# Several parts of the last image under way at once in the normalisation, the inverse DFT and the token layers

## The chip, the cores and the metric

The kernel runs as one program on one core of a Trainium2 chip. A core has a matrix engine (PE, with its weight loads shown as PEld), a vector engine (DVE), an activation engine (ACT), a general engine (POOL) and a queue engine (SP), which here issues all transfers between the memory of the chip (DRAM) and the on-chip buffer (SBUF). PE writes its results into PSUM, eight banks of 512 float32 per partition; DVE and ACT read them from there. The metric is the time of one execution on the device in microseconds.

## What is computed

The input is 4 images of 64 x 64 points with 96 channels. Four layers follow one another: two with a scan along the image in four directions, two with attention and a feed-forward part on the 4096 points as tokens.

```python
x = x + L0(group_norm(x))      # 192 inner channels
x = x + irfft2(L1(rfft2(x)))   # 64 x 33 frequencies, 384 inner channels
t = x.reshape(4, 4096, 96)
for layer in (2, 3):
    t = t + attn(norm(t)); t = t + ffn(norm(t))
# L0, L1: xz = x @ W; conv 3x3; silu; four scans with 16 states;
#         y = norm(sum of the four + skip) * silu(z); y @ out_w
# attn: q, k, v of 6 heads; ((q k^T) * 16**-0.5) v, no softmax; @ Wff + bff
# ffn: float8 (5 exponent bits, 2 of mantissa) factors, float16 sums,
#      relu between the two products
```

As attention has no softmax, the products can be taken in another order: the kernel forms one 97 x 97 matrix G = Xn^T Xn over all tokens of the image (96 channels and a column of ones), and from it and the weights one 97 x 96 matrix `wo`. Each token then needs only `xn @ wo`. G needs every normalised token before the first token can go on.

## The kernel before

`build` (line 1203) first prepares the first pair of images, then runs `scans` (line 480), which walks through all the scan steps of both scan layers: two phases for layer 0 (image pairs) and four for layer 1 (one image each). In `scans` the instructions of PE, DVE, ACT and POOL stand in an order written out by hand. The other work, for instance the normalisation after a scan, the inverse DFT and the token layers of an earlier image, runs as side tasks: generators that `Env.step` (line 83) moves on by one step where `slot` finds room. `E.defer` puts an eviction at the head of the next step.

When the scans of image 3 are through, nothing is left to run beside what still has to be done for that image: `alone(tail, end1, 3).finish()` (line 1288). This environment has `wide=4` and a PSUM pool of eight banks under one tag; the side tasks in the scans have `wide=1` and one bank. Outside the scans the order of the instructions in each engine's queue is set by a planner, which takes the code's order as priority. `end1` (line 1260) does three things one after another:

- `Block.gated` (line 350). The 33 rows of frequencies come in blocks of 8, 8, 6, 6 and 5 (`cfg.rows`), and a block in tiles of two rows. `load` (line 364) brings a tile: the scan results of the two row-wise directions `yt[:, 0]`, of the two column-wise ones `yt[:, 1]` by one transfer per row, and the scan's input `ut`; two tiles are buffered. Per tile PE multiplies `ut` with the skip weights (line 394) and adds the transposed four directions in the same bank (line 400), and ACT copies the bank into the block's `y` (line 410). Per block follow the mean by a product on PE (414), the subtraction on DVE (417), the square on ACT (420), the variance on PE (424), logarithm and exponential on ACT (427, 428), two multiplications on DVE (431, 436), and `out1` (line 899): for each row three products with `wo` (912), a copy for two rows (919), one store for the block into `att` (921). The buffers `y`, the gate `z` and the square `sq` exist once.
- `inverse` (line 982). Three groups of 32 channels, one after the other: two loads of `att` into `at` (998), 64 products `piv` in four banks (1013) with a copy each (1018), then two banks of `pio` (1029), the addition of the image from before the layer (1032), and the stores to `x1` (1034). The next group's `at` is loaded ahead; `v` exists once.
- `tokens` (line 1041). `x` holds the image as 32 tiles of 128 tokens. For each of the two layers: eight weight loads (1107 to 1118) with casts to float8 (1121, 1123); `layer_norm` (1058) over all tokens in four parts of eight tiles, the parts overlapping one another; G (`pg`, 1128) and the small products to `wo` (`small`, 1098); attention in eight groups of four tiles (transposition `pt` 1149, copy `xt` 1151, product `pao` 1155, addition 1157); the second `layer_norm`; the feed-forward part in eight groups (transposition `ptf` 1164, cast `x8` 1166, three products `ph` 1172 with copies 1173, bias and relu 1176, cast `h8` 1179, product `pfo` 1184, copy `y16` 1192, two additions 1194 and 1198). At the end one store of the whole image (1199).

`together` (line 111) gives several generators one step each in turn. Before, only the preparation of the first pair uses it.

Of the kernel before, what the change touches and what calls it, by code (L numbers as in the profile page):

```python
# [21 lines left out]
C, P = 3, 128  # L22
# [101 lines left out]
class Block:  # L124
# [225 lines left out]
    def gated(self, E, g, io, out_proj):  # L350


        nc, cfg = self.nc, self.cfg
        yn, yo = io["y"][cfg.nat], io["y"][1 - cfg.nat].rearrange("k (w r) c -> r w k c", r=cfg.NR)
        u, gz = io["u"][cfg.nat], io["gz"]
        with E.pool(f"{cfg.pre}nm{g}") as sp:
# [3 lines left out]
            tiles = [  # L360
                (b, i, r + i, min(2, n - i)) for b, (r, n) in enumerate(cfg.rows) for i in range(0, n, 2)
            ]

            def load(b, i, r, n):
                nm = f"{cfg.pre}_{g}_{r}"
                yt = sp.tile([P, 2, 2, C * P], F32, name=f"yt_{nm}", tag="yt", bufs=2)
# [5 lines left out]
                ut = sp.tile([P, C, P], F32, name=f"ut_{nm}", tag="ut", bufs=2)  # L372
                nc.sync.dma_start(out=ut[:, :, : n * 64], in_=u[:, :, r * 64 : (r + n) * 64])
                return yt, ut

            todo = iter(tiles)
            nxt = load(*next(todo))
            yield
            yield
            yield  # L380
            for b, (r, nr) in enumerate(cfg.rows):
                n = nr * 64
                nm = f"{cfg.pre}_{g}_{r}"
                z = sp.tile([P, C, 512], F32, name=f"zb_{nm}", tag="zb")
                nc.sync.dma_start(out=z[:, :, :n], in_=gz[:, :, r * 64 : r * 64 + n])
                y = sp.tile([P, C, 512], F32, name=f"yb_{nm}", tag="yb")
                for i in range(0, nr, 2):
                    m = min(2, nr - i) * 64
                    yt, ut = nxt
                    more = next(todo, None)  # L390
                    nxt = load(*more) if more else None
                    ps = E.psum(f"py_{nm}_{i}")[:, : C * P].rearrange("p (c t) -> p c t", c=C)
                    for c in range(C):
                        nc.tensor.matmul(
                            ps[:, c, :m], self.skip[:, c, :], ut[:, c, :m], start=(c == 0), stop=False
                        )
                    yield
                    for c in range(C):
                        for k in range(4):
                            nc.tensor.matmul(  # L400
                                ps[:, c, :m],
                                yt[:m, k // 2, k % 2, c * P : (c + 1) * P],
                                self.ident[:m, :m],
                                start=False,
                                stop=(c == C - 1 and k == 3),
                                is_transpose=True,
                            )
                        if c < C - 1:
                            yield
                    E.defer(lambda i=i, m=m, ps=ps, y=y: nc.scalar.copy(y[:, :, i * 64 : i * 64 + m], ps[:, :, :m]))  # L410
                    yield
                pm = E.psum(f"pm_{nm}")
                for c in range(C):
                    nc.tensor.matmul(pm[:, :n], self.mean_w, y[:, c, :n], start=(c == 0), stop=(c == C - 1))
                    yield
                for c in range(C):
                    nc.vector.tensor_tensor(y[:, c, :n], y[:, c, :n], pm[:, :n], ALU.subtract)
                yield
                sq = sp.tile([P, C, 512], F32, name=f"sq_{nm}", tag="sq")
                nc.scalar.activation(sq[:, :, :n], y[:, :, :n], AF.Square)  # L420
                yield
                pv = E.psum(f"pv_{nm}")
                for c in range(C):
                    nc.tensor.matmul(pv[:, :n], self.mean_w, sq[:, c, :n], start=(c == 0), stop=(c == C - 1))
                    yield
                ln = sp.tile([P, 512], F32, name=f"ln_{nm}", tag="ln")
                nc.scalar.activation(ln[:, :n], pv[:, :n], AF.Ln, bias=self.eps)
                nc.scalar.activation(pv[:, :n], ln[:, :n], AF.Exp, scale=-0.5)
                yield
                for c in range(C):  # L430
                    nc.vector.scalar_tensor_tensor(
                        y[:, c, :n], y[:, c, :n], self.lnw[:, c : c + 1], pv[:, :n], ALU.mult, ALU.mult
                    )
                yield LATE
                for c in range(C):
                    nc.vector.scalar_tensor_tensor(
                        y[:, c, :n], y[:, c, :n], self.lnb[:, c : c + 1], z[:, c, :n], ALU.add, ALU.mult
                    )
                yield
                yield from out_proj(E, sp, wo, y, r, nr)  # L440
# [429 lines left out]
def out0(images, ins, x0):  # L870


    def task(E, blk, sp, wo, y, r, nr):
        nc = E.nc
        PI = blk.cfg.PI
        tok = slice(r * 64, (r + nr) * 64)
# [105 lines left out]
def inverse(E, cst, att, x, b, x1):  # L982
# [5 lines left out]
    with E.pool(f"fi{b}") as sp:  # L988
# [5 lines left out]
        def load(c0):  # L994
            a = sp.tile([2 * HH, WP, G], F32, name=f"at_{b}_{c0}", tag="at", bufs=2)
            nc.gpsimd.memset(a[:, WF:, :], 0.0)
            for r in range(2):
                nc.sync.dma_start(
                    out=a[r * HH : (r + 1) * HH, :WF, :], in_=att[:, :, r * CH + c0 : r * CH + c0 + G]
                )  # L1000
            return a

        nxt = load(0)
        yield
        yield
        for c0 in range(0, CH, G):
# [395 lines left out]
```

## Time and profile before

| what | value |
|---|---|
| runs | 12100.39, 12104.8, 12110.57 us; median 12104.8 |
| profiled execution | 12108.82 us, of which its span is 12106.9 |
| mean granted PE clock | 0.87 of full |
| PE busy | 9441.0 us (78% of the span) |
| DVE busy | 10572.7 us (87%) |
| ACT busy | 9071.5 us (75%) |
| POOL busy | 8900.0 us (74%) |
| DRAM traffic | 1221.74 MB read, 236.50 MB written |

The page of the profile gives the busy time of each engine, also as digits in 40 equal slices of 302.7 us (a 9 is 90% busy or more; PEclk is the clock granted to PE in tenths). A window cuts out a stretch of microseconds from the span's start. A row of the timeline has the start, the length, the engine, the line of the code, the operation, output<-input with shapes, the number of merged instructions (x8), and in brackets how long the engine had stood idle before and what ended that. A row of the waits names who waited for whom, with total time, number of times, and the longest. Idle time of an engine that is not on the path to the end costs nothing.

### The profile page before, as it was taken

Reading aid. Unit: us, or ns where it says so; the run is one execution under the profiler, and the core shown is the slowest. Engines: PE = TensorE matmul, PEld = TensorE weight load, DVE = VectorE, ACT = ScalarE, POOL = GpSimd, SP = SyncE. Lnnn points to the kernel's source line nnn. Section 1 sums busy time; section 2 is a strip of 40 time slices with the busy share of each in tenths; the row PEclk is TensorE's granted clock in tenths of the full one; section 3 lists DMA queues with packets and bytes.
Section 4 is the critical chain, followed back from the end, with each engine's and each line's share of the span. In section 5 each row is a group of like instructions: output and inputs, shape, how many; then the busy total and the mean of one; then the engine's idle time right before and its main releaser. Section 6 shows DMA issues by size and latency. Waiting matters only on the chain. (4 is left out here: it accounts for less than half of the span.)

```text
span 12106.9 us, 164888 instructions
## 1 busy us (share of the span) xinstructions
PE 9441.0 (78%) x54800; PEld 6783.4 (56%) x54800; DVE 10572.7 (87%) x10183; ACT 9071.5 (75%) x18534; POOL 8900.0 (74%) x7074
## 2 busy tenths in 40 slices
PE   5677777777788778777888888788778877887765
PEld 2455555555666556556665565565556555565544
DVE  6899999999999999998879888988989899899854
ACT  3778888898778888887667777777777677777733
POOL 2888889888778888987668877877667766676630
PEclk8889999989889989998879889888878877898886
DMA  5554444556555445445543443444224422452231
GB/s 142 123 135 115 119 125 112 134 157 158 146 143 117 129 130 128 129 132 154 144 120 112 130 123 116 152 128 115 85 91 145 118 82 88 135 132 89 82 103 36
DMA packets 1270447, 1469.07 MB, mean 121 GB/s; under 512 B 496023, under 2 KB 1033823, under 8 KB 1260119
## 3 DMA queue, kind: packets, MB, share of 16 engines
q1 hardware_dynamic: 1269591, 1458.53, 44.1%
q8 instruction: 431, 7.06, 0.2%
q14 instruction: 425, 3.48, 0.1%
HBM read 1221.74 MB, written 236.50 MB: 120 GB/s over the span
## 5 line engine op out<-in xcount | busy, mean ns | idle before, releaser
L636 POOL TENSOR_TENSOR hy_l<-du_l,bc_l 128x512 f32<-128x512 f32 (+2 forms) x3456 | 3956.4, 1165 | 2266.6 <-DVE hcy_l L807 1206.7
L789 POOL TENSOR_TENSOR hcx_l<-hx_l,bc_l 128x1024 f32<-128x1024 f32 (+2 forms) x1616 | 3524.5, 2181 | 279.6 <-DVE hx_l L643 244.1
L593 ACT ACTIVATE bx_l<-dut_l,bt_l 128x192 f32<-128x192 f32 (+2 forms) x6272 | 2771.7, 498 | 0.1
L665 PE MATMUL acc_l<-ident,hcx_l 128*128 128x128 f32 (+1 forms) x12000 | 1885.7, 306 | 357.1 <-POOL hcx_l L789 353.3
L665 PE MATMUL acc_l<-ident,hcy_l 128*128 128x128 f32 (+1 forms) x11994 | 1850.5, 302 | 381.9 <-DVE hcy_l L807 378.5
L618 ACT ACTIVATE ax_l<-delta_l,l_alog 128x512 f32<-128x512 f32 (+2 forms) x3456 | 2139.3, 667 | 0.0
L665 PEld LDWEIGHTS acc_l<-ident,hcy_l 128*128 128x128 f32 (+1 forms) x11994 | 1550.1, 156 | 945.6 <-DVE hcy_l L807 571.3
L665 PEld LDWEIGHTS acc_l<-ident,hcx_l 128*128 128x128 f32 (+1 forms) x12000 | 1545.3, 157 | 852.5 <-POOL hcx_l L789 615.0
L807 DVE TENSOR_TENSOR hcy_l<-hy_l,bc_l 128x1024 f32<-128x1024 f32 (+2 forms) x1615 | 1950.7, 1208 | 43.0
L643 DVE TENSOR_TENSOR_SCAN hx_l<-ax_l,state_l,b_l 128x512 f32<-128x512 f32 (+2 forms) x1648 | 1786.8, 1125 | 222.8 <-PE b_l L613 142.1
L643 DVE TENSOR_TENSOR_SCAN hy_l<-b_l,state_l,hy_l 128x512 f32<-128x512 f32 (+2 forms) x1648 | 1789.7, 1121 | 143.8 <-ACT b_l L618 122.4
L618 ACT ACTIVATE b_l<-delta_l,l_alog 128x512 f32<-128x512 f32 (+2 forms) x1912 | 1200.4, 628 | 881.4 <-DVE hx_l L643 839.3
L613 PE MATMUL b_l<-ident,bx_l 128*128 128x128 f32 (+1 forms) x6718 | 1184.5, 303 | 408.3 <-DVE hy_l L643 193.5
L618 ACT ACTIVATE ab_l<-delta_l,l_alog 128x512 f32<-128x512 f32 x1321 | 909.3, 688 | 700.3 <-DVE hx_l L643 668.7
L613 PEld LDWEIGHTS b_l<-ident,bx_l 128*128 128x128 f32 (+1 forms) x6718 | 825.8, 152 | 905.8 <-DVE hy_l L643 296.7
L643 DVE TENSOR_TENSOR_SCAN hy_l<-ab_l,state_l,hy_l 128x512 f32<-128x512 f32 x961 | 1177.1, 1260 | 97.0 <-ACT ab_l L618 62.0
L643 DVE TENSOR_TENSOR_SCAN hx_l<-ax_l,state_l,ab_l 128x512 f32<-128x512 f32 x962 | 1177.5, 1265 | 95.6 <-PE ab_l L613 66.3
L613 PE MATMUL ab_l<-ident,bx_l 128*128 128x128 f32 x5288 | 903.3, 306 | 454.2 <-DVE hy_l L643 218.0
L656 POOL COPY state_l<-hx_l 128x2 f32<-128x2 f32 x1344 | 1114.3, 829 | 0.0
L613 PEld LDWEIGHTS ab_l<-ident,bx_l 128*128 128x128 f32 x5288 | 653.5, 154 | 799.4 <-DVE hy_l L643 298.5
L272 PE MATMUL pc_l<-pad_l,l_dg 128*128 128x512 f32 (+2 forms) x1656 | 796.5, 569 | 77.9 <-ACT uh_l L250 72.2
L176 PE MATMUL pi_l<-xi_l,l_wi 96*128 96x384 f32 (+6 forms) x912 | 469.0, 629 | 248.2 <-DMA xi_l<-xn 94.8
(193 smaller groups left out, 11970.2 us busy)
## 6 DMA issues: line engine op xcount, KB each, us to landing
bc_l<-l_xd_l SPq DMA_DIRECT2D x1536, 256.0 KB
bc_l<-l_xd_l SPq DMA_DIRECT2D x384, 512.0 KB
bc_l<-l_xd_l SPq DMA_DIRECT2D x384, 384.0 KB
us_l<-l_u SPq DMA_DIRECT2D x96, 768.0 KB
l_y<-y_l SPq DMA_DIRECT2D x288, 256.0 KB
bc_l<-l_xd_l SPq DMA_DIRECT2D x192, 320.0 KB
yt_l<-l_y SPq DMA_DIRECT2D x264, 192.0 KB
yt_l<-l_y SPq DMA_DIRECT2D x128, 384.0 KB
```

Of the source, the lines that this page charges most:

```text
L176: self.nc.tensor.matmul(out[i * cfg.PI : (i + 1) * cfg.PI, :n], wi[:, ki, half, :], xin[:, max(i, ki), :n], start=(ki == 0), stop=(ki == c ...
L272: nc.tensor.matmul(pc[:, : n * 64].rearrange("p (r w) -> p r w", w=64), diag[:, t, :], pad[:, r - p0 + dy : r - p0 + dy + n, dx : dx + 64] ...
L593: nc.scalar.activation(t[:n, b, :, ch], z.dut[:n, b, :, ch], AF.Copy, scale=z.bt[:n, b, m : m + 1])
L613: nc.tensor.transpose(pb[:, t : t + n], st.z.bx[st.q, j][:n, b, st.c], ident[:n, :n])
L618: nc.scalar.activation(out, z.delta[:, st.c, : z.S], AF.Exp, scale=z.blk.A[:, st.c, z.k, n : n + 1])
L636: nc.gpsimd.tensor_tensor(st.hy[:, j, :S], st.z.du[:, st.c, :S], st.z.b[st.q][:, j, :S], ALU.mult)
L643: nc.vector.tensor_tensor_scan(h[:, j, : z.S][:, ::step], a[:, : z.S][:, ::step], b[:, : z.S][:, ::step], 0.0 if z.first else z.state[st.c ...
L656: copy(z.state[st.c][:, n0 : n0 + 2].rearrange("p (j o) -> p j o", o=1), h[:, :, e : e + 1])
L665: nc.tensor.matmul(z.acc[st.c][:n, b, :], hc[:, j, t : t + n], ident, start=(n0 + j == 0 and b == 0), stop=(n0 + j == NST - 1 and b == 0), ...
L789: nc.gpsimd.tensor_tensor(hcx[:, :, :S], hx[:, :, :S], z.c[q][0][:, :, :S], ALU.mult)
L807: nc.vector.tensor_tensor(hcy[:, :, :S], st.hy[:, :, :S], z.c[q][1][:, :, :S], ALU.mult)
```

## The change

With `E.wide` over 1, that is for image 3 after the scans alone:

- `gated` is cut into three workers (`W = min(E.wide, 3)`). Worker `w` takes blocks w, w+3; all go in turns through `together`. Each has its own `yt`, `ut`, `zb`, `yb`, `sq`, `ln` and `ab` by a number in the tag, and loads its own next tile ahead.
- `inverse` loads all three channel groups first and runs them in turns, each with its own `v` and `xr`.
- `tokens` is opened before `inverse`, up to its first yield: constants, the ones of `xn` and the weight loads of both layers stand there, in buffers for two layers. The casts of both layers follow after the load of `x`. The tokens go through each layer as four parts of eight tiles (two groups of four): a part does attention for its two groups, its norm, the feed-forward part for its two groups, and, in layer 2, the norm for layer 3; in layer 3 it stores its result. The four parts go in turns. The first norm is done likewise. Between the layers G still needs all parts.

With `wide=1` (images 0 to 2) the steps stay, but for the weights of a token layer, whose eight loads are now issued together ahead of the four casts, and those of layer 2 ahead of the load of `x`; there is one yield more. The PSUM pool, the matrix products and the data moved are as before; the image's store is cut in four.

```diff
     def gated(self, E, g, io, out_proj):
+        W = min(E.wide, 3)
...
-                yt = sp.tile([P, 2, 2, C * P], F32, name=f"yt_{nm}", tag="yt", bufs=2)
+                yt = sp.tile([P, 2, 2, C * P], F32, name=f"yt_{nm}", tag=f"yt{b % W}", bufs=2)
...
+            def worker(w):
+                blocks = list(enumerate(cfg.rows))[w::W]
+                todo = iter([(b, i, r + i, min(2, n - i)) for b, (r, n) in blocks for i in range(0, n, 2)])
+                nxt = load(*next(todo))
+                yield
+                yield
+                yield
+                for b, (r, nr) in blocks:
+                    z = sp.tile([P, C, 512], F32, name=f"zb_{nm}", tag=f"zb{w}")
...
+                    yield from out_proj(E, sp, wo, y, r, nr, w)
+            yield from together([worker(w) for w in range(W)], W)
...
 def inverse(E, cst, att, x, b, x1):
+    W = min(E.wide, CH // G)
...
+        def channels(c0, a, w):
+            v = sp.tile([2 * WP, G, HH], F32, name=f"v_{b}_{c0}", tag=f"v{w}")
...
+        if W > 1:
+            loads = [load(c0) for c0 in range(0, CH, G)]
+            yield from together([channels(w * G, a, w) for w, a in enumerate(loads)], W)
...
 def tokens(E, ins, consts, ident, x1, b, out):
+    A, Q, W = CH + 1, 8, E.wide
...
+        def weights(ly):
+            nm, w, bufs = f"{b}_{ly}", {}, min(W, 2)
...
+                t = w[name] = sp.tile(shape, F32, name=f"{name}_{nm}", tag=name, bufs=bufs)
+                src = ins[f"l{ly}_{name}"]
+                nc.sync.dma_start(out=t, in_=src.to_broadcast([P, CH]) if name == "b2" else src)
+            yield w
+            for name in ("w1", "w2", "b1", "b2"):
+                t = w[name]
+                r = sp.tile(list(t.shape), F8, name=f"q{name}_{nm}", tag=f"q{name}", bufs=bufs)
+                yield LATE
+                nc.vector.tensor_copy(r, t, saturate=False)
...
+        loads = [weights(ly) for ly in (2, 3)]
+        ws = [next(loads[0])] + ([next(loads[1])] if W > 1 else [])
+        yield
         x = sp.tile([P, NT, CH], F32, name=f"tok_{b}", tag="tok")
         nc.sync.dma_start(out=x, in_=x1.rearrange("(p t) c -> p t c", t=NT))
+        yield
+        yield
+        for load in loads[: len(ws)]:
+            yield from load
...
+        def layer_norm(nm, p):
+            t0, w = p * Q, p % W
+            yield LATE
+            s = sp.tile([P, 2, Q], F32, name=f"lns_{nm}_{p}", tag=f"lns{w}")
+            m, v = s[:, 0, :], s[:, 1, :]
+            xs, xq = x[:, t0 : t0 + Q, :], xn[:, t0 : t0 + Q, :CH]
+            nc.vector.tensor_reduce(m, xs, AX.X, ALU.add)
+            nc.vector.tensor_scalar(m, m, 1.0 / CH, None, ALU.mult)
+            nc.vector.tensor_tensor(
+                xq, xs, m.rearrange("p (t o) -> p t o", o=1).to_broadcast([P, Q, CH]), ALU.subtract
+            )
+            yield
+            sq = sp.tile([P, Q, CH], F32, name=f"lnq_{nm}_{p}", tag=f"lnq{w}")
+            nc.scalar.activation(sq, xq, AF.Square)
+            yield LATE
+            nc.vector.tensor_reduce(v, sq, AX.X, ALU.add)
+            yield
+            nc.scalar.activation(v, v, AF.Ln, bias=eps, scale=1.0 / CH)
+            nc.scalar.activation(v, v, AF.Exp, scale=-0.5)
+            for t in range(Q):
+                nc.scalar.activation(xn[:, t0 + t, :CH], xn[:, t0 + t, :CH], AF.Copy, scale=v[:, t : t + 1])
+                if t == 3:
+                    yield
...
+        def part(ly, p, wo, q):
+            nm, w = f"{b}_{ly}", p % W
+            groups = range(p * Q // 4, (p + 1) * Q // 4)
+            for g in groups:
+                yield from attend(nm, g, w, wo)
+            yield from layer_norm(nm + "f", p)
+            for g in groups:
+                yield from feed(nm, g, w, q)
+            if ly == 2:
+                yield from layer_norm(f"{b}_3a", p)
+            else:
+                t = slice(p * Q, (p + 1) * Q)
+                nc.sync.dma_start(out=out[b].rearrange("(p t) c -> p t c", t=NT)[:, t], in_=x[:, t])
+
+        parts = range(NT // Q)
+        if W > 1:
+            yield from together([layer_norm(f"{b}_2a", p) for p in parts], W)
         for ly in (2, 3):
...
+            if W > 1:
+                yield from together([part(ly, p, wo, q) for p in parts], W)
+                continue
...
         def end1(E, b):
...
+            rest = tokens(E, ins, consts, ident, x1[b], b, out)
+            if E.wide > 1:
+                yield next(rest)
             yield from inverse(E, consts, att, x0[b], b, x1[b])
-            yield from tokens(E, ins, consts, ident, x1[b], b, out)
+            yield from rest
```

`attend` and `feed` hold the bodies of the former loops over the groups (lines 1147 to 1158 and 1162 to 1198), step for step, with tags numbered by part (`xt0`, `x80`, `h160`, ...); with `wide=4` `xt` and `x8` have one buffer per part where there were two. `norm_all` is the former `layer_norm` and stays for `wide=1`.

## The prediction

> **What bounds the kernel now.** The page comes first: its 40 slices show where the engines are full.
>
> ```profile
> span 12106.9 us, 164888 instructions
> ...
> PE   5677777777788778777888888788778877887765
> ...
> DVE  6899999999999999998879888988989899899854
> ACT  3778888898778888887667777777777677777733
> ```
>
> VectorE is at 9 tenths nearly throughout and falls only in the last two slices; that tail is the work of image 3, after the scans. The edit's new ways run only there (`wide=4`), so I cut the span at the tail's stages: normalisation (lines 350-440), inverse transform (982-1035), token layers (1041-1200).
>
> ```profile
> core 0: us, PE busy (x) PEld busy (x) DVE busy (x) ACT busy (x) POOL busy (x), PEclk, DMA share, GB/s
> 11650.00:11838.00 188.00, 119.95 (x564) 88.13 (x564) 25.48 (x45) 28.14 (x50) 0.10 (x1) 0.80 0.45 114
> 11838.00:11890.00 52.00, 35.13 (x408) 26.16 (x408) 4.14 (x7) 7.23 (x13) 2.76 (x4) 0.87 0.78 100
> 11890.00:12107.00 217.00, 121.31 (x640) 87.97 (x640) 114.80 (x208) 97.21 (x262) 0.00 (x0) 0.55 0.06 20
> ```
>
> The columns are the stretch, its length, busy time of PE, PEld, DVE, ACT and POOL, granted clock, DMA share, GB/s. No engine fills a stage but PE in the inverse: 35 of 52 us, of which 9 are the first load. The token layers run PE at a mean clock of 0.55. So the tail is chains; the waits of the first stage say which.
>
> ```profile
> DVE yb_l L417 <- PE pm_l L414: 128.0, 5, 35.2
> ...
> PE py_l L394 <- DMA ut_l<-l_u: 31.2, 8, 9.4
> ...
> PE po L912 <- DVE yb_l L436: 18.6, 5, 4.3
> ...
> PE pv_l L424 <- ACT sq_l L420: 15.5, 5, 3.6
> ```
>
> Columns: total us, times, longest. PE stands 31 us for a tile's loads and 34 us in the middle of blocks, for the mean, the variance and the product with the gate. The timeline tells why nothing fills this.
>
> ```profile
> 11671.64 0.48 ACT L410 COPY yb_l<-py_l 128x384 f32<-128x384 f32 x1 [2.55 <-PE py_l L400]
> ...
> 11695.53 9.63 PE L912 MATMUL po<-l_wo,yb_l 128*64 128x192 f32 x48 [4.17 <-DVE yb_l L436]
> ...
> 11705.09 0.94 PE L394 MATMUL py_l<-ut_l,l_skip 128*128 128x128 f32 x6
> ```
>
> At 11671.64 the tile whose buffer block 1's first tile takes is through PE, and SP issues that load; some 7 us later, as for the tiles before, it is there. Yet its matmuls (L394) begin only at 11705.09, behind block 0's last output product (L912). In the token layers:
>
> ```profile
> 11964.28 1.05 PE L1164 MATMUL ptf<-ident,xn 128*96 128x128 f32 x4
> ...
> 11966.24 1.46 PE L1172 MATMUL ph<-x,qw 96*128 96x512 fp8e5 x3 [0.91 <-DVE x L1166]
> ...
> 11966.68 0.95 DVE L1079 TENSOR_REDUCE lns_3a<-tok 128x8 f32<-128x768 f32 x1
> 11966.89 1.56 ACT L1173 CAST h<-ph 128x512 f16<-128x512 f32 x3 [1.89 <-PE ph L1172]
> ...
> 11969.62 0.95 DVE L1179 CAST h<-h 128x1536 fp8e5<-128x1536 f16 x1
> ...
> 11970.63 1.14 PE L1184 MATMUL pfo<-qw,h 128*128 128x96 fp8e5 x12 [2.93 <-ACT lnq_3a L1091]
> ...
> 12005.83 6.03 PE L1128 MATMUL pg<-xn 128*97 128x97 f32 x48
> ```
>
> DVE takes layer 3's reduction (L1079) ahead of five feed groups that the code has before it, but PE keeps the code's order: the 48 `pg` matmuls, whose inputs are scaled in part from 11976, run after the last `pfo`. I reckon on this: PE in the code's order, DVE and ACT taking the earliest ready. A feed group without norms beside it costs 6.55 us (`ptf` at 12059.57 and 12066.12), through PE, DVE and ACT in turn.
>
> **The change part by part.** The profiled execution took 12108.8 us (span 12106.9), 4.0 above the median of the runs; I sum against it and take 4.0 off at the end.
>
> *Normalisation, 188 us.* Blocks have 8, 8, 6, 6 and 5 rows; three workers take 0+3, 1+4 and 2 in turns. Nothing is removed: 17 tiles of 960 KB and 2.1 MB of gate still come in. The first turns ask for 11 tiles (rows 0-21) at once: with the weight 13.2 MB. Slices of 3 us with a DMA share near 1 moved 220 to 265 GB/s; at 250 that is 53 us, so the last tile is through PE near 11709. PE (11 x 4.05 cold) hides under it. Left for PE: mean and variance of the two long blocks 4 x 2.84, a variance of 2.2, 22 rows of output product at 1.2 (9.63 for 8) 26.9, six tiles at 2.0, mean and variance 8.0, 11 rows 13.8: 74 us. The stalls of 3.6 and 4.2 us per block are now filled by another worker's steps, except what one worker waits for behind the other on DVE: 5 in the first round, 9 in the second, and 4 for a third tile's load: 18. End near 11801 instead of 11838: **-36**. Bounds: -20, if DMA gives 225 and half of the 74 us runs at the half clock; -67, if PE's 120 busy us become the length.
>
> *Weights ahead of the inverse.* The mask and 16 weight loads move in front of the inverse's on SP. Rows of 0.28 to 0.43 us each make 5.5; the wait for `att` (2.9) covers a part. If their memory comes free with the tile buffers, before the last block ends, it costs 0; if only then, and with stalls such as `wqt`'s 3.85, +8. I take **+2**, nearer to the early release, since the first buffers are long read. The casts, which stood in front of the first norm's subtraction at 11903.11, then run while x lands; that gain is in the norm below.
>
> *Inverse, 51 us.* PE was full but for the start (384 `piv` in 24.6, 24 `pio` in 11.0), so three parts win at most 3. In turns PE needs all three inputs at once: each pair of loads is 528 KB at 139 to 144 GB/s, 3.7 us, while two `piv` steps give 2.1 of work: stalls of 1.7 to 2.7, twice, with the first part's next `piv` and ACT's copies queued behind. The results now all leave at the end, 12 writes of 128 KB, 10.5 us at 150 GB/s beside 11.0 of `pio`. **+4**, from -3 to +10.
>
> *First token norm.* From 11895.62 (x landed) to the last `pg` at 11919.66 are 24.0. After: DVE 4 x 2.0, one reduction 0.95, ACT 4 x (0.30+0.21+8 x 0.29) = 11.4, last `pg` 2.3: 22.6. **-1.4**, from -7 (the whole wait for weights gone) to +2.
>
> *Layers.* The four parts go in lockstep, as PE keeps their turns. Attention: until part 0's second addition, eight transposes and five products: 15.9 us by cold rows (0.87, 1.78), some 8 warm (0.47; the product warm, 0.9, is an estimate from half of 1.78). Layer 2's first `pt` row (0.60) is warm, the second (1.06) cold, so I take the middle: 12, with copy and addition. Then the norm, which before lay beside the other groups' attention: DVE 4 x 2.55 and 0.95, ACT 4 x 1.68 and 4 x 1.17: 22.6 to the first feed copy. Feed, first round of four groups: nine copies 5.2 until part 0's last, DVE 4 x 1.31, then 4 x (1.02+0.6): 39.6. Second round: copies to 43.7, DVE 5.2 and 4.1: 53.0. Layer 3 takes 12+53 = 65, was 82.7 (12018.09 to 12100.76): **-17.7**. Layer 2 has the next norm behind it, formerly beside the feed: 8.0+0.95+11.4+2.3, so 87.6, was 92.4: **-4.8**. Together, bounds -75 (DVE's 115 busy us nearly set the length of the token layers) and +5 (attention cold, no copy moved up).
>
> A rule that speaks against this part: the Trainium skill's Perfetto Trace Analysis, Optimization Strategy, advises interleaving regimes whose busiest engines differ. The edit sets like beside like and takes norm and attention apart. By that rule the layers would gain near 0.
>
> Another speaks for it: the skill's TensorE: Matmul & The Clock Gate, Why this matters for your kernels, wants PE busy some 4 us on end for the full clock. This trace's attention, 80% busy in pieces of 3 us, stood at 0.50; four transposes and four products on end may pass. By the rule attention ends at 8, without it at 16, and the sum shifts by 8 either way.
>
> *Buffers.* Each part's own `lnq`, `xt`, `x8`, `h16`, `h8`, `y16` cost nothing; `xt` and `x8` fall to one per part, and their next use is a whole round of four later; were it not, a group would wait one copy, 0.6.
>
> *Output.* Four stores instead of one; the last part needs 384 KB behind the last addition, the others leave some 1 us apart before it: **-2**, from 0 to -3.
>
> *Images 0 to 2* take the old paths. Only their weight loads are issued in one block, and one step is added per image. Cost 0: SP's waits in the scans (3273 us for L573 on POOL) show loads standing ready early. Should that cover be gone, see the third rival.
>
> Sum: -36+2+4-1.4-17.7-4.8-2 = -56; 12108.8-56-4 = 12049.
>
> **Rivals.** *Queues fill far better than my lockstep.* For: DVE and ACT do reorder. Against: PE does not. Normalisation -60, inverse 0, layers -70, start and output -7: -137, 11968.
>
> *The turns stall as much as they hide.* PE in the code's order waits for whichever worker is last. For: eight waits on `ut` in a row that PE could not pass. Normalisation -20, weights +8, inverse +10, layers -8: -10, 12095.
>
> *Slower: SP blocks in the scans.* Of images 0 to 2, layer 3's `b2` load waits for layer 2's last addition and now stands directly behind it; the scan's broadcast loads queue behind. It decides once such a block outlasts the broadcast buffers, some two steps of 7.2 us (one scan step in the trace). Overcoming 56 and 24 more takes 27 us for each of three images, nearly four steps. Against: the longest wait row of L1118 is 1.1 us. 3 x 27 - 56 = +25: 12130.
>
> *The edit does nothing*, because DVE and ACT orders were already free: 12105. Against: the PE rows above.
>
> **How the numbers follow.** Chances: my case 0.54 (own range 12015 to 12082), better filling 0.18, stalls 0.13, nothing 0.07, slower 0.08. Telling a difference needs 0.2%, 24 us: faster takes my case, the first rival and a third of the stalls, 0.77; same 0.15; slower 0.08. The range goes from 11975, most of the first rival, to 12097, which takes in the stalls; outside are no change, slower, and an end of the first rival, 0.2.
>
> **What would show it.** In the normalisation: DMA share near 1 until about 11709 and the 17 `py` tiles no longer split by L912 alone; end near 11801. Inverse: two waits on `at` inside `piv`. Layers: four `pt` and four `pao` back to back at a higher clock; a hole in DVE while ACT scales; layer 3 near 65 us. My forecast is wrong if PE leaves the code's order, if layer times stay at 92 and 83, or if the stretch before 11650 changes by over 10 us.

## The result and the profile after

The changed kernel takes 12019.76 us (median of 4 runs, 12013.74 to 12022.29), the kernel before 12102.59 (4 runs, 12095.86 to 12110.57): a ratio of 0.9931, 95% interval 0.9913 to 0.9948, some 83 us less where 56 were forecast. The profiled execution took 12018.33 us. Its page:

```profile
span 12016.6 us, 164869 instructions
...
PE   6677777777778878778888888888777887787765
...
DVE  6899999999989998998889888888989889899974
ACT  3778888888778888887667777777777777777753
```

The slices look like those of before except at the end: in the last but one DVE stands at 7 tenths and ACT at 5, where they had 5 and 3. The tail is shorter, the scans in front of it are as full as they were. The stages of the tail in windows (stretch, length, busy PE, PEld, DVE, ACT, POOL, granted clock, DMA share, GB/s):

```profile
11631.00:11773.00 142.00, 102.91 (x564) 81.16 (x564) 25.17 (x46) 27.65 (x50) 0.82 (x2) 0.87 0.61 150
11798.00:11845.00 47.00, 36.71 (x408) 26.38 (x408) 3.95 (x6) 7.05 (x12) 0.00 (x0) 0.83 0.70 86
11851.00:12016.00 165.00, 93.77 (x640) 71.17 (x640) 107.12 (x196) 94.31 (x262) 0.00 (x0) 0.69 0.03 10
```

The numbers of instructions are those of before on PE. The first stage fell from 188 to 142 us, the last from 217 to 165 at a clock of 0.69 instead of 0.55. Between the first two windows lie 25 us in which PE does nothing. The inverse did not get shorter: its window here starts only with the first product, which the table below allows for. By landmarks that both traces have, against the prediction's terms:

| stretch | before | after | change | forecast |
|---|---|---|---|---|
| start to the issue of the scans' last store | 11650.9 | 11631.7 | -19.2 | 0 |
| from there to the last `att` store (normalisation) | 187.8 | 141.4 | -46.4 | -36 |
| to the first `piv` (weights ahead) | 8.8 | 24.9 | +16.1 | +2 |
| to the issue of the tokens' load (inverse) | 41.8 | 47.3 | +5.5 | +4 |
| first norm, x landed to last `pg` | 24.0 | 20.7 | -3.3 | -1.4 |
| layer 2, `wo` to last `pg` | 92.2 | 78.3 | -13.9 | -4.8 |
| layer 3, `wo` to last addition | 82.4 | 55.7 | -26.7 | -17.7 |
| last addition to the end | 6.2 | 3.7 | -2.5 | -2 |

Behind the scans these make -71.2. Five terms gained more than forecast, one lost far more, and 19 us come from a stretch that was to stay. The experiments ask first whether those 19 us belong to the edit, then what each term consists of.

How the normalisation runs now, in windows of 10 us and in PE's waits:

```profile
11680.00:11690.00 10.00, 6.74 (x39) 5.86 (x38) 0.00 (x0) 0.96 (x2) 0.00 (x0) 0.74 1.10 261
11690.00:11700.00 10.00, 10.00 (x34) 5.63 (x33) 2.56 (x5) 1.64 (x2) 0.00 (x0) 0.92 0.90 216
11700.00:11710.00 10.00, 8.54 (x29) 4.31 (x29) 9.19 (x17) 6.45 (x9) 0.00 (x0) 1.00 0.01 4
...
11720.00:11730.00 10.00, 10.00 (x62) 8.24 (x61) 0.00 (x0) 2.43 (x6) 0.00 (x0) 1.00 0.12 26
```
```profile
PE py_l L395 <- DMA ut_l<-l_u: 29.9, 10, 9.5
PE po L916 <- DVE yb_l L437: 4.7, 1, 4.7
PE pv_l L425 <- ACT sq_l L421: 3.8, 2, 2.3
```

The transfers stand at full share for 60 us after the scans' end and at 0.8 to 1.0 for 8 more, and PE waits for them; the last tile of the first turns is through PE 62 us after the scans' end (58 forecast). From 11690 to the end of the last product at 11772.1 PE is busy for 70.7 us and idle for 11.4, at a mean clock of 0.95. The 31 us of waiting for loads are still there (29.9), but the 34 us that PE had stood in the middle of blocks are 8.5 now. One timeline row shows the workers at it: the output products of three blocks run as 132 instructions without a hole, 0.17 us each, where before one block's 48 came alone at 0.20.

```profile
11707.77 22.12 PE L916 MATMUL po<-l_wo,yb_l 128*64 128x192 f32 x132
```

The weights, in the timeline of SP, and what they did to PE:

```profile
11771.51 1.61 SPq L925 DMA_DIRECT2D att<-ab  x2
11773.22 0.54 SPq L1064 DMA_DIRECT2D tk_mask<-in_head_mask  x1
...
11776.25 4.59 SPq L1077 DMA_DIRECT2D w<-in_l_w  x2
...
11784.53 5.39 SPq L1077 DMA_DIRECT2D w<-in_l_w  x2
11789.97 0.90 SPq L1077 DMA_DIRECT2D b<-in_l_b  x2
...
11791.86 10.31 SPq L1003 DMA_DIRECT2D at<-att  x6
```
```profile
11798.03 2.23 PE L1014 MATMUL piv<-ih,at 128*64 128x64 f32 x32 [25.91 <-DMA at<-att]
...
11801.81 2.23 PE L1014 MATMUL piv<-ih,at 128*64 128x64 f32 x32 [1.56 <-DMA at<-att]
...
11806.17 20.24 PE L1014 MATMUL piv<-ih,at 128*64 128x64 f32 x320 [2.13 <-DMA at<-att]
```

Not one weight is issued before the last `att` store, and from 11773.22 to 11790.87 SP does nothing but issue them; `at` comes behind. The two waits inside `piv` are the forecast ones. That the memory was not free earlier shows in one of the first instructions that write into the token layers' pool:

```profile
11772.18 0.06 DVE L1062 MEMSET tk_eps<- 128x1 f32 x1 [10.75 <-PE po L916]
```

It needs nothing from `po`, and yet it waits for the normalisation's last product.

Layer 3 in the timeline:

```profile
11956.67 1.91 PE L1172 MATMUL pt<-ident,xn 128*97 128x128 f32 x16
...
11958.42 3.71 PE L1178 MATMUL pao<-wo,xt 97*128 97x96 f32 x32
...
11964.79 0.55 DVE L1180 TENSOR_TENSOR tok<-tok,pao 128x384 f32<-128x384 f32 x1 [2.06 <-PE pao L1178]
11965.44 0.95 DVE L1145 TENSOR_REDUCE lns_3f<-tok 128x8 f32<-128x768 f32 x1
...
11980.03 5.13 ACT L1159 ACTIVATE xn<-xn,lns_3f 128x96 f32<-128x96 f32 x19
...
11985.08 5.85 ACT L1195 CAST h<-ph 128x512 f16<-128x512 f32 x12
...
11985.67 4.20 DVE L1198 TENSOR_SCALAR h<-h,b 128x512 f16<-128x512 f16 x9 [2.29 <-ACT h L1195]
```

Four parts' transpositions run as 16 in 1.91 us (0.48 for four; before 0.60 and then 1.06), the products as 32 in 3.71. Attention until part 0's second addition takes 8.2 us, the norm to the first feed copy 19.7, the rest 27.8. Between 11977.8 and 11985.7 DVE has but four casts to do while ACT scales: the hole that the prediction named.

### The profile page after: what moved, and what is told of

Read it like the earlier page. It is cut to its first block, busy times and chain, and to the rows that moved or that the text cites. A ratio compares the mean times of both kernels' runs of the same rounds, so it can differ in the third digit from the quotient of the medians.

```text
span 12016.6 us, 164869 instructions
## 1 busy us (share of the span) xinstructions
PE 9377.0 (78%) x54800; PEld 6736.8 (56%) x54800; DVE 10565.3 (88%) x10183; ACT 9068.6 (75%) x18534; POOL 8904.7 (74%) x7074
```

## The experiments

All ratios are to the kernel before, timed beside each experiment on the same chip; its median there was 12099.0, 12093.2, 12098.2 and 12094.7 us. The stage lengths come from each run's profile by the landmarks above. They repeat well: layer 3 took 55.7 us in every run that left it as in the changed kernel, the normalisation in three workers 137 to 141.5.

**narrow and oldscan: do the scans' 19 us belong to the edit?** `narrow` sets all three widths to 1, `oldscan` keeps the new tail and gives images 0 to 2 the old order of the weights.

In `narrow`:

```diff
-        W = min(E.wide, 3)
+        W = 1
...
-    W = min(E.wide, CH // G)
+    W = 1
...
-    A, Q, W = CH + 1, 8, E.wide
+    A, Q, W = CH + 1, 8, 1
...
-            if E.wide > 1:
-                yield next(rest)
```

In `oldscan`, inside `tokens`:

```diff
-        ws = [next(loads[0])] + ([next(loads[1])] if W > 1 else [])
-        yield
+        ws = []
+        if W > 1:
+            ws = [next(w) for w in loads]
+            yield
...
-            if len(ws) < ly - 1:
-                ws.append(next(loads[1]))
-                yield from loads[1]
+            if W == 1:
+                q = {}
+                ws.append(q)
...
+                    nc.sync.dma_start(out=t, in_=src.to_broadcast([P, CH]) if name == "b2" else src)
+                    if name not in ("w1", "w2", "b1", "b2"):
+                        continue
+                    r = sp.tile(shape, F8, name=f"q{name}_{nm}", tag=f"q{name}")
+                    yield LATE
+                    nc.vector.tensor_copy(r, t, saturate=False)
...
```

> All three stages of image 3 go one part at a time again, as in the kernel before; what stays of the change is that the eight weight loads of a token layer are issued together (images 0 to 3) and one step is added per image. Theory A, this reordering shortens the scans by the 19 us that the two profiles differ by at the scans' end: the last store of scan results is issued near 11631 instead of 11650, and the time is 12103 - 19 = 12084. Theory B, the 19 us is how executions of such a program differ from one another: the time is 12103 within 8, the scans' end anywhere from 11630 to 11660.

> The changed kernel for image 3, but for images 0 to 2 the weight loads and steps stand as in the kernel before, so every engine's order is that of before up to the end of the scans. Theory A (the scans' 19 us belong to the edit): 12020 + 19 = 12039, the scans' end near 11650. Theory B (variation): 12020 within 8.

Measured: `narrow` 12094.5 us over 11 runs, ratio 0.9996 (0.9987 to 1.0006); `oldscan` 12023.5, ratio 0.9938 (0.9925 to 0.9950), where the changed kernel has 0.9931. Theory A wanted 0.9984 and 0.9947; the first lies outside its interval, the second inside but near the edge. By the times alone A seems to fall. But they are the sum of scans and tail, and the tails differ: from the scans' last store to the end it is 456.1 us in the kernel before, 465.2 in `narrow`, 384.9 in the changed kernel and 380.6 in `oldscan`. What the profiled execution of `narrow` gained in front it lost behind.

The end of the scans does not decide it either: it came at 11650.9 in the kernel before and 11641.2 in `oldscan`, and anywhere from 11606.9 to 11639.8 in the twelve profiles with the new order (`narrow` 11625.6, below the range of theory B). Part of that is older than the edit. Up to the load of image 0's mask every engine has the same instructions in the same order in all fourteen profiles, and yet that load is issued between 8319.7 and 8352.7 us. From there to the scans' last store, where the two orders differ, the kernel before takes 3299.5 us and `oldscan` 3301.0; the twelve profiles with the new order, the changed kernel's with 3286.7 and `narrow`'s with 3290.6 among them, take 3283.3 to 3293.0, 3288.8 in the mean. The two groups do not overlap. So of the 19.2 us 6.4 lie in front of the first instruction that differs and are how executions differ from one another, and 12.8 lie behind it. By the means the order of the weights, with the one step more, is worth 11 us.

The waits of DVE in the scans from 8300 us on tell where they come from, in the kernel before, in `oldscan` and in the changed kernel:

```profile
DVE qw L1121 <- DMA w<-in_l_w: 24.7, 3, 9.3
```
```profile
DVE qw L1257 <- DMA w<-in_l_w: 26.0, 3, 9.4
```
```profile
DVE qw L1083 <- DMA w<-in_l_w: 1.2, 1, 1.2
```

In the old order the first cast of a weight came up in DVE's queue before its load had landed, once for each of images 0 to 2, and DVE, the engine at 9 tenths, stood still for 6 to 9 us each time. With the weights issued ahead of x and the casts later, that wait is all but gone. About half of these 24 us arrives at the scans' end; where the rest is lost again was not followed up. The rival in which SP blocks in the scans falls with `narrow`.

**gated: the normalisation alone.** The inverse and the tokens with `W = 1`, the tokens opened after the inverse.

> Of the three stages only the normalisation goes in three workers; the inverse and the token layers of image 3 go one part at a time, the tokens are opened after the inverse. From the scans' end to the last store of the normalised result: 140 us, as in the changed kernel, against 187.7 before, so -47; the forecast had -36. Time 12103 - 47 = 12056 if the scans are as before, 12037 if the scans' 19 us belong to the edit. If the workers' gain only shows because the later stages follow at once, the time is above 12067.

Measured: 12048.3, ratio 0.9958 (0.9946 to 0.9971), -51 us; the stage took 141.3 us (-46.5). The stage's gain stands by itself, two thirds of the tail's 71 us. The -51 us is not this stage alone: images 0 to 2 have the new order here too, and the tokens' load now stands behind eight weight loads, 48.0 us after the first `piv` instead of 41.8.

**gated2: two workers.** One line, on the kernel `w_own_pool` below.

```diff
-        W = min(E.wide, 3)
+        W = min(E.wide, 2)
```

> The kernel with own memory for the weights (11997.7), but the normalisation goes in two workers (blocks 0, 2, 4 and 1, 3) instead of three. Theory K, the first 60 us are bound by the loads and PE is nearly full after them, so a second worker does most of it: the stage takes 138 to 146 us, the time is up to 12006. Theory L, each worker hides a share of the stalls: of the 50 us that three gained over one (187.8 to 137.7) a quarter to a half is lost, 150 to 163 us and 12010 to 12023.

Measured: 12014.3, ratio 0.9934 (0.9918 to 0.9951; three workers there 0.9916). The stage took 156.1 us instead of 137.7: theory L. The waits of PE in it:

```profile
PE py_l L395 <- DMA ut_l<-l_u: 28.7, 10, 9.9
PE po L916 <- DVE yb_l L437: 9.9, 5, 3.1
PE pv_l L425 <- ACT sq_l L421: 7.6, 3, 2.8
```

The wait for loads is the same. The waits for DVE and ACT rose from 8.5 to 17.5, and PE's busy time from 101.1 to 109.7 us (clock 0.85 instead of 0.89). So the third worker is worth 18 us: half in stalls filled, half in PE's busy time, which is shorter at the higher clock. That the clock is higher because less stands between the products was not tried apart.

**w_own_pool and w_after_at: what the weights cost.** In `w_own_pool` weights and mask get a memory pool of their own, opened before `gated`, and the code of their loads moves into a step inside `gated`. In `w_after_at` they stay where they are in memory, but the code has the inverse's loads first.

`end1` steps `tokens` to the first new yield ahead of `gated`, and to the second (both layers' weights and the mask) from a step inside `gated`:

```diff
+        if W > 1:
+            wp = pools.enter_context(E.pool(f"tw{b}"))
+            yield
+            early = []
+            for ly in (2, 3):
...
+                    t = early[-1][name] = wp.tile(shape, F32, name=f"{name}_{b}_{ly}", tag=f"{name}{ly}")
+                    src = ins[f"l{ly}_{name}"]
+                    nc.sync.dma_start(out=t, in_=src.to_broadcast([P, CH]) if name == "b2" else src)
...
+            yield
+        sp = pools.enter_context(E.pool(f"tk{b}"))
...
+            for k, s in enumerate(
+                blk[1].gated(E, b, io, lambda E, *a: put(E, blk[1], *a))
+            ):
+                if E.wide > 1 and k == 135:
+                    next(rest)
+                yield s
```

In `w_after_at` both generators have one more yield, `tokens` ahead of the mask's load, `inverse` behind the loads of `at`:

```diff
                 yield next(rest)
-            yield from inverse(E, consts, att, x0[b], b, x1[b])
+                inv = inverse(E, consts, att, x0[b], b, x1[b])
+                yield next(inv)
+                yield next(rest)
+                yield from inv
...
```

> The changed kernel, but the sixteen weights and the mask of image 3 have memory of their own, taken before the normalisation, so that their loads need not wait for its buffers. Theory C (the loads, 17.7 us of issues on SP from the last att store on, stand in front of the inverse's loads and cost what they take): the first product of the inverse comes 9 us after the last att store instead of 26, and the time is 12020 - 17 = 12003. Theory D (the inverse has to wait for the att stores anyway, the loads cost the 2 us of the forecast): 12018. If the loads now stand before the normalisation's own loads and delay these: above 12020.

> The changed kernel (12019.8; inverse in turns, weights in the token layers' memory), but the weights and the mask are loaded behind the inverse's loads of att on SP's queue, and the memory they get is that of the normalisation as in the changed kernel. Theory C' (what costs is the place in SP's queue): the first product of the inverse 9 us after the last att store; the weights' 17 us now stand in front of the inverse's loads of the image and lie beside its first products, from the first product to the tokens' load 47 to 52 us: 12003 to 12008. Theory O (the loads of att also wait for memory or for the att stores as long as the weights take): 12018.

Measured: `w_own_pool` 11997.7, ratio 0.9916 (0.9903 to 0.9930), from the last `att` store to the first `piv` 8.7 us; `w_after_at` 12001.9, ratio 0.9922 (0.9905 to 0.9938), 8.8 us, but the inverse took 51.1, as its loads of the image now stand behind the weights. Theory C and C' hold; D and O fall. What the pair does not separate is memory and place: `w_own_pool` changes both. SP in it:

```profile
11686.68 0.27 SPq L1074 DMA_DIRECT2D wqkv<-in_l_wqkv  x1
...
11697.76 4.48 SPq L1074 DMA_DIRECT2D w<-in_l_w  x2
...
11703.24 0.43 SPq L1076 DMA_DIRECT2D tk_mask<-in_head_mask  x1
...
11758.64 1.61 SPq L925 DMA_DIRECT2D att<-ab  x2
...
11762.96 10.52 SPq L1003 DMA_DIRECT2D at<-att  x6
```

The same loads take as long, 17 us, but in a gap of SP in the normalisation, where nobody waits for them.

**own_inv: the inverse one group after the other**, on `w_own_pool`.

```diff
 def inverse(E, cst, att, x, b, x1):
-    W = min(E.wide, CH // G)
+    W = 1
```

> The kernel with own memory for the weights (11997.7), and the inverse's three channel groups one after the other as in the kernel before. Theory E, the turns cost here (PE waits twice for at, the stores leave together at the end): from the first product to the load of the tokens 41.8 us, as before, instead of 47.3, and the time is 11998 - 5.5 = 11992. Theory F, the stores' end is set by the transfers and the turns cost nothing: 47 us again, 11998.

Measured: from the first `piv` to the tokens' load 41.7 us; ratio 0.9905 (0.9890 to 0.9920). Theory E, by the profile: the two ratios' intervals overlap, 5.6 us is less than they tell apart. The times alone, 18 us lower than `w_own_pool`, were taken on another chip. PE's `piv` and `pio` alternate in blocks, after the first without a wait for `at`, and the stores leave beside the next group's `piv`:

```profile
11758.04 8.27 PE L1014 MATMUL piv<-ih,at 128*64 128x64 f32 x128 [9.89 <-DMA at<-att]
...
11769.67 3.06 SPq L1035 DMA_DIRECT2D x<-xr  x4
11770.44 8.21 PE L1014 MATMUL piv<-ih,at 128*64 128x64 f32 x128
```

**att_serial: attention group by group**, norms and feed-forward in four parts as before, on `w_own_pool`.

```diff
-            for g in groups:
-                yield from attend(nm, g, w, wo)
             yield from layer_norm(nm + "f", p)
...
+                for g in range(NT // 4):
+                    yield from attend(nm, g, g // 2, wo)
                 yield from together([part(ly, p, wo, q) for p in parts], W)
```

> The kernel with own memory for the weights (11997.7), but the eight attention groups of a token layer go one after the other (four transposes, copy, four products, addition), as in the kernel before, and only the norms and the feed-forward parts go in four. Theory I, the attention's gain is the PE's clock and the hidden copies: from wo to the second addition of part 0 it is now past all of the others, the copies stand between the PE's pieces, the transposes run at 0.22 us and not 0.12, the block takes some 16 to 20 us instead of 8: 10 more for each layer, 12018. Theory J, the attention does not matter, since the norm's chain behind it starts at the first part anyway: 12000.

Measured: 12005.1, ratio 0.9927 (0.9912 to 0.9942); layer 2 took 86.1 us and layer 3 65.3, against 76.5 and 55.7: theory I, 9.6 for each (the time rose by less than that, as the scans of these executions ended earlier: 11606.9 in the profile against 11622.6). The first 20 us of its layer 3 in a window, and rows of its timeline:

```profile
11922.00:11942.00 20.00, 15.84 (x68) 13.95 (x67) 7.83 (x13) 7.17 (x18) 0.00 (x0) 0.52 0.00 0
```
```profile
11924.66 1.06 PE L1196 MATMUL pt<-ident,xn 128*97 128x128 f32 x4
...
11926.45 2.02 PE L1202 MATMUL pao<-wo,xt 97*128 97x96 f32 x8 [0.73 <-ACT xt L1198]
```

and the attention of the changed kernel:

```profile
11957.10:11965.40 8.30, 8.30 (x78) 8.30 (x77) 2.80 (x6) 4.10 (x8) 0.00 (x0) 1.00 0.00 0
```

The granted clock is 0.52 with PE stopping 0.7 us for each copy and 1.00 with no stop; four transpositions take 1.06 us against 0.48. When it rises can be seen in the changed kernel just ahead of this, where PE runs the `pg` products without a gap from 11947.47 on:

```profile
11947.47:11951.00 3.53, 3.53 (x21) 3.53 (x22) 0.00 (x0) 3.39 (x13) 0.00 (x0) 0.50 0.02 5
11951.10:11953.87 2.77, 2.77 (x32) 2.60 (x31) 0.00 (x0) 0.00 (x0) 0.00 (x0) 1.00 0.00 0
```

The Trainium skill's TensorE: Matmul & The Clock Gate, Why this matters for your kernels, which wants PE busy some 4 us on end, agrees with the changed kernel, whose clock was full 3.6 us after PE had begun to run without a gap. `att_serial` has the same `pg` products in front, but in the window above, busy for 15.84 of 20 us in pieces of 3 us, its clock is back at one half.

**stagger and stag_norm: unlike beside unlike.** `stagger` (on `w_own_pool`) lets part p begin 3 p steps later, by these lines at the head of `part`; `stag_norm` (on `own_inv`) has them behind the attention, ahead of `layer_norm(nm + "f", p)`.

```diff
+            for _ in range(3 * p):
+                yield
```

> The kernel with own memory for the weights (11997.7), but part p of the four token parts begins 3 p steps later, so that the norms of one part (DVE, ACT) stand beside the attention and the feed-forward products of another (PE). Theory G, mixing regimes fills more: the hole of some 8 us in which DVE waits while ACT scales all four parts' tokens goes, layer 3 falls from 55.8 to about 50 and layer 2 from 76.5 to about 71: 11987. Theory H, like beside like is as good because the four parts' chains already fill DVE and ACT, and a later start is only added at the end: layer 3 at 58 or more, 12000 to 12010.

> The kernel with own memory for the weights and the inverse one group after the other, with the attention of the four parts in turns as before, but part p's norm and feed-forward begin 3 p steps later. The first staggered run lost the full clock in the attention, so it did not test the mixing alone. Theory G, mixing the regimes fills DVE's hole: layer 3 at 50 to 53. Theory H, like beside like is as good: 56 or more, since each later start is added at the end.

Measured: `stagger` 11995.0, ratio 0.9917 (0.9903 to 0.9932), layer 2 75.4 us, layer 3 66.5. Theory H by layer 3 (58 or more; the time fell short of its 12000), but probably for another reason than it gives: part 0's attention then ran alone, and the clock in layer 3 was 0.53 instead of 0.72. `stag_norm` keeps the attention together: 11978.6, ratio 0.9898 (0.9884 to 0.9913), layer 2 68.2 us and layer 3 54.8, against 75.9 and 55.7 in `own_inv`. Layer 2 gains 7.7 us, as G's mechanism has it; in layer 3 neither theory holds (50 to 53, or 56 and more). That the late starts give back there what they fill is my reading, not shown. ACT in layer 2 of `stag_norm` now has scalings of one part between copies of another:

```profile
11868.80 0.91 ACT L1183 ACTIVATE xn<-xn,lns_2f 128x96 f32<-128x96 f32 x3
11869.60 0.58 ACT L1219 CAST h<-ph 128x512 f16<-128x512 f32 x1
11870.07 1.18 ACT L1183 ACTIVATE xn<-xn,lns_2f 128x96 f32<-128x96 f32 x4
11871.60 0.59 ACT L1219 CAST h<-ph 128x512 f16<-128x512 f32 x1 [0.35 <-PE ph L1218]
```

**half_scale: ACT's scalings shared with DVE**, on `own_inv`.

```diff
-            for t in range(Q):
+            late = xq[:, 4:, :]
+            vb = v[:, 4:].rearrange("p (t o) -> p t o", o=1).to_broadcast([P, Q - 4, CH])
+            nc.vector.tensor_tensor(late, late, vb, ALU.mult)
+            for t in range(4):
                 nc.scalar.activation(xn[:, t0 + t, :CH], xn[:, t0 + t, :CH], AF.Copy, scale=v[:, t : t + 1])
...
```

> The kernel with own memory for the weights and the inverse one group after the other (ratio 0.9905 to before), and in each part's norm the scaling of four of the eight token tiles done by DVE in one instruction (128x384, the reductions and subtractions of 128x768 took 0.95 us, so some 0.55) instead of four by ACT (0.27 each). Theory M, the norm of the four parts is bound by ACT's 32 scalings while DVE waits (some 10.7 us from the first square root on, of which ACT's scalings are 8.6): 4 x 1.1 less on ACT, 3.5 to 4 us less for each of the four norms of the tail, -14 in all: layer 3 near 52, ratio 0.989 to 0.990. Theory N, the DVE work of the feed-forward part behind it is the bound and only starts later or earlier by nothing: layer 3 at 55.7.

Measured: 11976.6, ratio 0.9899 (0.9885 to 0.9914); first norm 18.2 us (21.4 in `own_inv`), layer 2 71.1 (75.9), layer 3 53.2 (55.7): -10.5 of the -14 expected. Theory M by the profile, three quarters of its size; the two ratios' intervals overlap. DVE takes the scalings in what was its hole, 0.5 us each:

```profile
11942.41 1.48 DVE L1184 TENSOR_TENSOR xn<-xn,lns_3f 128x384 f32<-128x384 f32 x3
```

**best: all together**, the lines of `half_scale` and of `stag_norm` on `own_inv`.

> All that gained, together: own memory for the weights, the inverse one group after the other, half of the scalings on DVE, the norms and feed-forward parts begun 3 p steps apart behind an attention in turns. From the scans' end to the end of the span the single steps gave 358.8 us without the last two, 10.5 less with the half scalings (first norm 3.2, layer 2 4.8, layer 3 2.5), 8.6 less with the steps apart (layer 2 7.7, layer 3 0.9). If the two fill different holes: 340, ratio to before near 0.988. If they fill the same hole (DVE waiting while ACT scales): 348 to 350, ratio 0.989 to 0.990, no better than either.

Measured: 11971.3, ratio 0.9897 (0.9881 to 0.9914); from the scans' last store to the end 350.4 us, against 350.9 in `half_scale`, 348.8 in `stag_norm`, 358.8 in `own_inv` and 384.9 in the changed kernel. That is the second case expected, that the two last steps fill the same hole; layer 3 even rose to 58.7, for which no run gives the reason. Any of the three beats both the kernel before and the changed one (0.9931), by some 40 us more; between them the runs do not choose.

## Why the prediction was right, and where it was wrong

The sign, the mechanism of the tail and the range held; the forecast was 29 us too high. The tail gained 71 us where 56 were forecast, images 0 to 2 some 11 to 13 where nothing was. Term by term:

- *Normalisation*, -36 against -46.4. The first phase was right: bound by transfers, 62 us for 58. (The gate is 3.2 MB in all; the 2.1 MB of the text are those of the first 22 rows, which the sum of 13.2 MB has right.) The term that was mis-sized is "stalls 18" behind it. From 11690 to 11772.1 PE was busy for 70.7 us (the 74 of the sum) and idle for 11.4: three workers waited less for one another than supposed, two (`gated2`, 17.5) as supposed.
- *Weights*, +2 against +16.1: the term of the tail that was mis-sized most, and outside its own bound of +8. Two parts of it failed. "The early release, since the first buffers are long read": `tk_eps` waited 10.7 us for the last `po`, and the mask followed the last store. And the 5.5 us of issues were summed from rows of 0.28 to 0.43, while each pair of `w1` and `w2` took 4.6 to 5.4. The trace of before had this already, in image 3's own loads:

```profile
11894.71 5.38 SPq L1118 DMA_DIRECT2D w<-in_l_w  x2
```

`w_own_pool`, by own memory and an earlier place, and `w_after_at`, by a later place alone, each took the 16 us in front of the inverse away.
- *Inverse*, +4 against +5.5, with its two waits (1.56 and 2.13) and its stores at the end; `own_inv` undid it.
- *Layers*, -22.5 against -40.6. In layer 3 the attention took 8.2 where I had the middle between cold and warm, 12; the norm 19.7 for 22.6, as the reductions and subtractions took 1.8 per part without the additions that I had put between them all; the feed-forward 27.8 for 30.4. `att_serial` shows the attention's part: 9.6 us a layer hang on its running in one piece.
- *The rule against this part* (the Trainium skill's Perfetto Trace Analysis, Optimization Strategy: interleave regimes with different busiest engines) was read as giving near 0; the measured -40.6 decides against that reading. It is not empty here: once the attention stayed together, putting norms beside other parts' feed-forward gave 7.7 us more in layer 2 and 0.9 in layer 3.
- *Images 0 to 2*, 0 against -12.8 between the two profiles (-11 by the means): the step that failed in kind. Its reason, that SP's waits on POOL show loads standing ready early, was true of the scan's loads, not of the weights: the trace of before has DVE waiting 24.7 us for them in the scans. "The stretch before 11650" did change by over 10 us, which the prediction had named as a sign of being wrong, and rightly so; only its size at the scans' end (19 us) holds 6 us of chance.
- *Rivals.* That the queues fill far better came true in part: the layers went over half of the way to its -70, the normalisation to -46 of its -60, and the weights ate the gain. That the turns stall came true for the inverse alone. SP blocking in the scans and "nothing" fell.

That the sum came out within 29 us owes something to luck, since errors cancelled: the weights cost 14 us more than forecast, the normalisation and the layers together 28 less.

What stays open: why only about half of DVE's saved waits in the scans reaches their end, and whether memory or place alone would have freed the weights.

## What to carry to other kernels

When a stage is a chain and several independent parts exist, run them in turns with own buffers, and count the workers: here the third was worth 18 us after the second. Keep PE's pieces of one kind together, since with a stop of 0.7 us for a copy between them the clock stood at half and a layer took 10 us more; then let the vector and scalar work of the parts drift apart. When loads are moved ahead, look in SP's timeline where their issues land and what stands behind them, and whether their memory is free by then. And measure a change in a long program from the first instruction that differs: what lies in front of it is chance, and what lies behind it need not be.

## What was not expected of the hardware

- With one order of instructions up to the scans' end, that end came between 11606.9 and 11639.8 us in twelve profiled executions, while stages of the tail repeated within 1 to 5 us. Most of the spread arises in the first 8300 us (33 us there); the 3290 us behind them repeated within 10, close enough to see an effect of 11 us that the end of the scans hides.
- The issue of two small weights (96x384 and 128x288 floats) held SP for 4.6 and 5.4 us in the changed kernel and for 2.9 and 4.5 in `w_own_pool`, beside 0.3 to 1.0 for most other weights.
